# Layer 3: four of 32 tiles of exponentials summed by accumulating DMA in place of three summed by products with ones on TensorE

## The chip, the core and the metric

The kernel runs on one core of a Trainium2 chip. The core has TensorE (PE: matrix products, from SBUF into PSUM), ScalarE (ACT: here the exponentials), VectorE (DVE: elementwise sums and scalings), GpSimd (POOL: here only constants and DMA issues at the start), SyncE (SP: issues DMAs) and 16 DMA engines that all the queues share. The metric is the device time of one execution in microseconds (us), the median of several.

## The reference

Four layers run over four images of 64 x 64 pixels with 64 channels, all in float32: a self-attention over the pixels (layer 0), a convolution block (layer 1), an attention over the columns of the feature map (layer 2), and a non-local block (layer 3), which is where the change is:

```python
def _L3_conv_ref(x, g_W, g_b, phi_W, phi_b, theta_W, theta_b, w_W, w_b, gamma, beta):
    B, H, W, C = x.shape
    N = H * W
    g_x = (jnp.einsum('bhwc,cd->bhwd', x, g_W) + g_b).reshape(B, N, INNER)
    phi_x = (jnp.einsum('bhwc,cd->bhwd', x, phi_W) + phi_b).reshape(B, N, INNER)
    theta_x = (jnp.einsum('bhwc,cd->bhwd', x, theta_W) + theta_b).reshape(B, N, INNER)
    f = jnp.einsum('bnd,bmd->bnm', theta_x, phi_x)
    f = jax.nn.softmax(f, axis=-1)
    y = jnp.einsum('bnm,bmd->bnd', f, g_x).reshape(B, H, W, INNER)
    w_y = jnp.einsum('bhwd,dc->bhwc', y, w_W) + w_b
    mean = jnp.mean(w_y, axis=(0, 1, 2))
    var = jnp.var(w_y, axis=(0, 1, 2))
    w_y = gamma * (w_y - mean) * jax.lax.rsqrt(var + EPS) + beta
    return x + w_y
```

With N = 4096 and INNER = 32, each image needs a 4096 x 4096 matrix of exponentials, its products with g, and the sum of each of its rows, by which the products are divided at the end.

## The kernel before, in words

Every layer is cut into items, and a loop in `run` issues them one after another. After item i come the pieces due at i: an item's exponentials are used by products that are due one or two items later. TensorE, ACT, DVE and POOL execute their instructions in exactly the order in which this program issues them; nothing is reordered later. A semaphore wait is added wherever an instruction needs another engine's result or overwrites what another engine still reads.

Layer 3 of an image (`layer3(b)`) is 64 items in two blocks (nb = 0 and 1) of 32 tiles (mc = 0 to 31). A block holds 2048 query pixels, and a tile has the exponentials of 128 key pixels against them, 128 x 2048 numbers in one of six rotating SBUF buffers (`ep`, six buffers). For tile n:

- `scores(n)`, line 1408: eight matmuls into two PSUM slots, then two exponentials of 128 x 1024 on ACT (lines 1413 and 1414) into the tile `e`.
- `products(n)`, issued two items later. Line 1443: four matmuls of `e` with g, accumulated over the block's 32 tiles in one PSUM bank, `y`. The row sums also need every tile added up. For that there are two ways: DVE adds the tile to `esum`, a buffer in `m.tg`, which each image has for itself (lines 1434 and 1436, 128 x 2048 per add), and TensorE multiplies tiles 9, 19 and 29 by ones into a second PSUM bank, `z` (line 1429). In the very last block of the program tiles 28 to 31 take TensorE's way. Tile 0 needs no add of its own, since the add of tile 1 takes both.
- At the end of a block ACT copies `y` out of its bank (line 1449). `totals` then has TensorE multiply `esum` by ones (`sums`, line 1455), which adds the partition sums to `z`. It is due four items after the block's last tile, or two items after it where layer 2 of a later image follows (images 0 and 1, second block). A logarithm and an exponential on ACT and three DVE instructions (`newton`, lines 1471 to 1473) make the reciprocal and divide, spread over the following items; then `close`, eleven items after, projects by W (line 1490), with ACT's bias (line 1503) and the statistics for the normalisation on DVE (line 1505).

In a block that follows another of the same image, the first add of the new block (line 1434) overwrites `esum`, so it waits for the `sums` of the block before it.

`new_acc` hands out two PSUM banks in turn; a block takes one for `y` and one for `z`. `xn` is a pool with a single 128 x 2048 buffer, used by layer 1's normalisation. Layer 3 of image 0 runs after layer 2 of image 1, that of image 1 after layer 2 of image 2, and layer 3 of images 2 and 3 run one after the other at the end. During image 2's first block, pieces of preparation for image 3 (`close2`, `open3`) are put between the items; the latter issues 16 DMAs on SP (`ph<-tg`).

Of the kernel before, what the change touches and what calls it, by code (L numbers as in the profile page):

```python
# [8 lines left out]
F32 = mybir.dt.float32  # L9
AF = mybir.ActivationFunctionType  # L10
ALU = mybir.AluOpType
# [680 lines left out]
def fast_path(ctx: ExitStack, tc: tile.TileContext, a: dict, out: bass.AP, bad):  # L692
    nc = tc.nc
# [10 lines left out]
    xn = ctx.enter_context(tc.tile_pool(name="xn", bufs=1))  # L704
# [10 lines left out]
    def new_ps():  # L715
        s = turn_of["slots"][turn_of["ps"] % len(turn_of["slots"])]
        turn_of["ps"] += 1
        return PS[:, bass.ts(s, 1024)]
# [4 lines left out]
    def new_acc():  # L723
        turn_of["acc"] += 1
        return PS[:, bass.ts(6 + turn_of["acc"] % 2, 512)]

    def new_e(name="e"):
        return ep.tile([128, 2048], F32, tag="e", name=name)

    def new_t(name="t"):  # L730
        return tp.tile([128, 1024], F32, tag="t", name=name)
# [8 lines left out]
    act = nc.scalar.activation  # L740
# [9 lines left out]
    def fetch_x(b, queues):  # L750
# [17 lines left out]
        out=gam0, in_=a["L0_conv_gamma"].rearrange("(o n) -> o n", o=1).to_broadcast([128, 1])  # L768
# [44 lines left out]
    for nm in names128:  # L813
        r = flat[nm].shape[0] // 128
        nc.sync.dma_start(
            out=rows[col[nm] : col[nm] + r, :], in_=flat[nm].rearrange("(r c) -> r c", r=r)
        )
    for nm in names64 + names32:
        n = flat[nm].shape[0]
        nc.sync.dma_start(  # L820
            out=rows[col[nm] : col[nm] + 1, :].rearrange("o (d n) -> o d n", n=n),
            in_=flat[nm].rearrange("(r d n) -> r d n", r=1, d=1).to_broadcast([1, 128 // n, n]),
# [523 lines left out]


    wys, early = {}, []
    small = {}
    held = []  # L1350

# [44 lines left out]
    def layer3(b):  # L1396
        m, first, last = im[b], len(items), b == B - 1
        es, st = {}, {}

        def scores(n):  # L1400
            nb, mc = n // 32, n % 32
            e = es[n] = new_e()
            tiles = [new_ps(), new_ps()]
            for kp in range(2):
                for c in range(2):
                    for i in range(2):
                        rows_ = slice(64 * kp + 32 * i, 64 * kp + 32 * i + 32)
                        mm(  # L1408
                            tiles[kp][64 * c : 64 * c + 64, bass.ts(i, 512)],
                            m.ph[rows_, 128 * mc + 64 * c : 128 * mc + 64 * c + 64],  # L1410
                            m.th[rows_, bass.ts(nb, 512)], start=True, stop=True,
                        )
            act(e[:, 0:1024], tiles[0], AF.Exp)  # L1413
            held.append(lambda: act(e[:, 1024:2048], tiles[1], AF.Exp))  # L1414
            if not (mc == 1 and (nb or last)):
                held.pop()()
            for fn in small.get(first + n, []):
                fn()

        def products(n):  # L1420
            nb, mc = n // 32, n % 32
            e, esum = es[n], m.tg[:, 2048:4096]
            if mc == 0:
                st["y"] = new_acc()
            if mc % 10 == 9 or (last and n >= 60):
                if mc == 9:
                    st["z"] = new_acc()
                for k in range(4):
                    mm(  # L1429
                        st["z"][32 * k : 32 * k + 32, :], ones[:, 0:32], e[:, bass.ts(k, 512)],  # L1430
                        start=mc == 9, stop=False,
                    )
            elif mc == 1:
                nc.vector.tensor_add(esum, es[n - 1], e)
            elif mc:
                nc.vector.tensor_add(esum, esum, e)  # L1436
            if last and n == 62:
                return
            if last and n == 63:
                sums()  # L1440
            for i in (n - 1, n) if last and n == 63 else (n,):
                for k in range(4):
                    mm(  # L1443
                        st["y"][32 * k : 32 * k + 32, :], m.gx[:, i % 32, :], es[i][:, bass.ts(k, 512)],
                        start=mc == 0, stop=i % 32 == 31,
                    )
            if mc == 31 and not (last and n == 63):
                st["yz"] = new_t("yz")
                nc.scalar.copy(st["yz"][:, 0:512], st["y"])
                if held:  # L1450
                    held.pop()()

        def sums():
            for k in range(4):
                mm(
                    st["z"][32 * k : 32 * k + 32, :], ones[:, 0:32],
                    m.tg[:, 2048 + 512 * k : 2560 + 512 * k], start=False, stop=True,
                )


        def log(cols):
            st["inv"] = st.get("inv") or new_t("inv")
            act(st["inv"][:, cols], st["z"][:, cols], AF.Ln)

        def exp(cols):
            act(st["inv"][:, cols], st["inv"][:, cols], AF.Exp, scale=-1.0)

        def newton(nb):
            yz, z, t = st["yz"], st["z"], st.pop("inv")
            r, d = t[:, 0:512], t[:, 512:1024]  # L1470
            nc.vector.tensor_mul(d, z, r)
            stt(d, d, -2.0, r, ALU.add, ALU.mult, accum_out=inv3[:, 2 * b + nb : 2 * b + nb + 1])
            stt(yz[:, 0:512], d, -1.0, yz[:, 0:512], ALU.mult, ALU.mult)

        def totals(n):
            sums()
            steps = [
                lambda: log(slice(0, 256)), lambda: log(slice(256, 512)),
                lambda: exp(slice(0, 256)), lambda: exp(slice(256, 512)), lambda: newton(n // 32),
            ]  # L1480
            for i, fn in enumerate(steps):
                if n == 63 and b < 2:
                    fn()
                else:
                    small.setdefault(first + n + 5 + min(i, 3), []).append(fn)

        def project(yz, ps, c0, cols):
            for k in range(4):
                s, jj = k // 2, k % 2
                mm(  # L1490
                    ps[64 * s : 64 * s + 64, 512 * jj : 512 * jj + c0], wo[32 * k : 32 * k + 32, :],
                    yz[32 * k : 32 * k + 32, cols], start=True, stop=True,
                )

        def close(nb):
            if b % 2 == 0 and nb == 0:
                wys["pair"] = new_big("wy") if b else new_pad("wy")
            if nb == 0:
                wys[b] = wys["pair"][:, bass.ts(b % 2, 2048)]
            ps = new_ps()  # L1500
            project(st["yz"], ps, 512, slice(0, 512))
            wy = wys[b][:, bass.ts(nb, 1024)]
            act(wy, ps, AF.Identity, bias=V("L3_conv_w_b"))
            for i in range(2):
                nc.vector.bn_stats(bst[:, b, nb, i, :], wy[:, bass.ts(i, 512)])

        def close_last():
            yz, inv, wy = new_t("yz"), new_t("inv"), wys[b][:, 1024:2048].rearrange("p (j n) -> p j n", j=2)
            for i in range(2):
                r = inv[:, bass.ts(i, 256)]  # L1510
                act(r, st["z"][:, bass.ts(i, 256)], AF.Ln)
                act(r, r, AF.Exp, scale=-1.0)
            early.append(begin_out(0))
            for i in range(2):
                cols, r, d = bass.ts(i, 256), inv[:, bass.ts(i, 256)], inv[:, 512 + 256 * i : 768 + 256 * i]
                nc.vector.tensor_mul(d, st["z"][:, cols], r)
                k = 2 * b + 1 + i
                stt(d, d, -2.0, r, ALU.add, ALU.mult, accum_out=inv3[:, k : k + 1])
                stt(yz[:, cols], d, -1.0, st["y"][:, cols], ALU.mult, ALU.mult)
                ps = new_ps()  # L1520
                project(yz, ps, 256, cols)
                act(
                    wy[:, :, cols], ps.rearrange("p (j n) -> p j n", j=2)[:, :, 0:256],
                    AF.Identity, bias=V("L3_conv_w_b"),
                )
            for i in range(2):
                nc.vector.bn_stats(bst[:, b, 1, i, :], wy[:, :, bass.ts(i, 256)])

        for n in range(64):
            items.append((lambda n=n: scores(n), 1.0))  # L1530
            at(first + n + 2, lambda n=n: products(n))
            if last and n == 63:
                at(first + n + 2, close_last)
            elif n % 32 == 31:
                at(first + n + (2 if n == 63 and b < 2 else 4), lambda n=n: totals(n))
                at(first + n + 11, lambda n=n: close(n // 32))
# [255 lines left out]
```

## Time and profile before

| | us |
|---|---|
| median of 4 runs | 2604.98 |
| lowest to highest | 2603.13 to 2605.3 |
| the profiled execution | 2604.95 |
| its span, first to last instruction | 2603.2 |
| granted TensorE clock, mean | 0.998 of full |

Busy time of each engine in stretches of layer 3, as the profile gives it (image 0's two blocks, then image 2's second and image 3's first):

| stretch, us | length | PE | DVE | ACT | POOL |
|---|---|---|---|---|---|
| 1519 to 1588 | 69 | 69.00 | 62.39 | 59.83 | 0.00 |
| 1588 to 1665 | 77 | 77.00 | 67.27 | 68.17 | 0.00 |
| 2350 to 2430 | 80 | 80.00 | 70.40 | 70.59 | 0.00 |
| 2430 to 2500 | 70 | 70.00 | 64.16 | 61.88 | 0.00 |

In the profile's rows PE is TensorE's matmuls and PEld its weight loads. A float32 matmul shows as two records, so four matmuls are eight records. Matmuls overlap each other and their ends are modelled, so one matmul's duration is longer than its share of TensorE's time; the distance between starts tells more. ACT's exponentials overlap a little as well: two in a row are 0.92 us apart at 1.02 us each. A row of the timeline gives the start, the duration, the engine, the line, the operation with its destination and sources, and how many instructions were merged into it; in brackets stands how long the engine was idle before it, and what ended that.

### The profile page before, as it was taken

The numbers are of one execution on the slowest core, as the hardware profiler recorded it, in microseconds if no ns is written. First come the engines' busy times: TensorE is split into PE (matmuls) and PEld (weight loads), VectorE is DVE, ScalarE is ACT, GpSimd is POOL, SyncE is SP. The second block draws the span as 40 slices with busy tenths as digits, with TensorE's granted clock in tenths as the row PEclk, the third lists the DMA queues.
The fourth block names the chain that finished last, engine by engine and source line by source line (L and its number), as shares of the span: only waits on it lengthen the run. The fifth ranks groups of instructions, "written<-read, shape, count | busy, mean of one in ns | idle before, by whom it ended". The sixth has DMA issues, their size and how long they took to land.

```text
span 2603.2 us, 55344 instructions
## 1 busy us (share of the span) xinstructions
PE 2572.2 (99%) x24477; PEld 871.8 (33%) x24477; DVE 1162.7 (45%) x1302; ACT 1769.1 (68%) x2814; POOL 14.3 (1%) x46
## 2 busy tenths in 40 slices
PE   9999999999999999999999999999999999999997
PEld 3343333333333345333333322233322333322223
DVE  2010266312672237613671168610088500098996
ACT  4666766666666676666656578756688655678885
POOL 2000000000000000000000000000000000000000
PEclk9999999999999999999999999999999999999999
DMA  3000000001000000010010000010000010010002
GB/s 75 1 18 1 17 18 2 17 2 33 1 2 17 17 18 1 1 33 18 1 33 18 17 1 2 2 34 1 18 2 1 9 26 1 1 34 2 1 2 67
DMA packets 24557, 36.75 MB, mean 14 GB/s; under 512 B 3724, under 2 KB 12149, under 8 KB 24309
## 3 DMA queue, kind: packets, MB, share of 16 engines
q1 hardware_dynamic: 23285, 32.03, 5.6%
q8 instruction: 194, 3.18, 0.5%
q0 software_dynamic: 704, 0.56, 0.1%
q10 hardware_dynamic: 320, 0.54, 0.1%
q14 instruction: 54, 0.44, 0.1%
HBM read 4.80 MB, written 4.19 MB: 3 GB/s over the span
## 4 chain that ended last, share of the span: by engine, by line
PE 96%; ACT 2%; DVE 1%; issue 0%; SPq 0%; DMA 0%; ACTq 0%; DVEq 0%
PE PS L1307 17%; PE PS L1289 17%; PE PS L1084 16%; PE PS L1058 16%; PE PS L1408 11%; PE PS L1443 10%; PE PS L1168 2%; PE PS L1429 1%; ACT e L1063 1%; PE PS L1026 1%; PE PS L1230 1%; PE PS L1253 1%; PE PS L1133 1%; PE PS L1387 1%; ACT q L1008 0%; PE PS L941 0%
## 5 line engine op out<-in xcount | busy, mean ns | idle before, releaser
L1063 ACT ACTIVATE e<-PS 128x1024 f32<-128x1024 f32 x512 | 523.7, 1023 | 327.2 <-PE PS L1058 284.7
L1297 ACT ACTIVATE e<-PS 128x1024 f32<-128x1024 f32 x512 | 516.8, 1025 | 292.6 <-PE PS L1289 289.4
L1084 PE MATMUL PS<-e,vq 64*64 64x512 f32 x4096 | 540.1, 591 | 0.0
L1058 PE MATMUL PS<-X,q 64*64 64x512 f32 x4096 | 537.3, 591 | 1.8 <-DVE X L942 1.7
L1436 DVE TENSOR_TENSOR tg<-tg,e 128x2048 f32<-128x2048 f32 x213 | 488.0, 2291 | 23.9 <-ACT e L1414 5.7
L1289 PE MATMUL PS<-ko 64*64 64x512 f32 x4096 | 469.3, 591 | 2.2 <-ACT ko L1271 1.7
L1307 PE MATMUL PS<-e,X 64*64 64x512 f32 x4096 | 464.2, 591 | 0.0
L1413 ACT ACTIVATE e<-PS 128x1024 f32<-128x1024 f32 x256 | 262.6, 1026 | 84.5 <-PE PS L1408 63.7
L1201 DVE SCALAR_TENSOR_TENSOR y<-pad,vec,y 128x1024 f32<-128x1024 f32 x240 | 308.1, 1284 | 8.2 <-ACT pad L1185 1.1
L1408 PE MATMUL PS<-tg,ph 32*64 32x512 f32 x4096 | 311.1, 613 | 0.5 <-ACT e L1413 0.5
L1443 PE MATMUL PS<-e,tg 128*32 128x512 f32 x2048 | 271.9, 603 | 0.0
L1414 ACT ACTIVATE e<-PS 128x1024 f32<-128x1024 f32 x256 | 261.6, 1022 | 0.0
L1058 PEld LDWEIGHTS PS<-X,q 64*64 64x64 f32 x4096 | 161.5, 133 | 279.0 <-issue 231.6
L1289 PEld LDWEIGHTS PS<-ko 64*64 64x64 f32 x4096 | 156.8, 133 | 289.8 <-issue 199.3
L1084 PEld LDWEIGHTS PS<-e,vq 64*64 64x64 f32 x4096 | 161.1, 133 | 272.5 <-issue 170.8
L1307 PEld LDWEIGHTS PS<-e,X 64*64 64x64 f32 x4096 | 155.6, 133 | 274.9 <-issue 271.4
L1071 DVE TENSOR_REDUCE sums<-zs 128x1 f32<-128x4 f32 x128 | 19.8, 155 | 374.3 <-ACT e L1063 374.2
L1315 DVE TENSOR_TENSOR ph<-ph,PS 128x512 f32<-128x512 f32 x16 | 11.0, 687 | 391.7 <-ACT ph L1314 391.7
L1408 PEld LDWEIGHTS PS<-tg,ph 32*64 32x64 f32 x4096 | 80.6, 130 | 217.2 <-issue 119.7
L1443 PEld LDWEIGHTS PS<-e,tg 128*32 128x32 f32 x2048 | 43.6, 108 | 200.9 <-issue 196.9
L1297 ACT ACTIVATION_READ_ACCUMULATOR e<-PS 128x1 f32 x512 | 106.6, 208 | 0.0
L1063 ACT ACTIVATION_READ_ACCUMULATOR e<-PS 128x1 f32 x512 | 99.6, 195 | 0.1
(193 smaller groups left out, 948.1 us busy)
## 6 DMA issues: line engine op xcount, KB each, us to landing
xn<-t SPq DMA_DIRECT2D x64, 128.0 KB
ph<-tg SPq DMA_DIRECT2D x64, 128.0 KB
ko<-ko SPq DMA_DIRECT2D x16, 256.0 KB
xr<-in_x_dram SPq DMA_DIRECT2D x13, 256.0 KB
q<-q SPq DMA_DIRECT2D x12, 256.0 KB
out_dram<-o SPq DMA_DIRECT2D x8, 256.0 KB
out_dram<-o SPq DMA_DIRECT2D x4, 512.0 KB
xr<-in_x_dram ACTq DMA_DIRECT2D x2, 128.0 KB
```

Source lines behind the costliest of these rows:

```text
L1058: mm(ps[64 * c : 64 * c + 64, bass.ts(r, 512)], m.q[rows_, 128 * t + 64 * c : 128 * t + 64 * c + 64], x[rows_, bass.ts(g, 512)], start=Tru ...
L1063: act(es[g // 2][:, bass.ts(g % 2, 1024)], ps, AF.Exp, bias=SHIFT0, accum_out=zs[:, g : g + 1],)
L1084: ins = mm(PS[64 * s : 64 * s + 64, 2048 + 512 * j : 2560 + 512 * j], vq[rows_, :], es[j // 2][rows_, k : k + 512], start=t == 0 and i < 2 ...
L1201: stt(y1, win, wt, y1, ALU.mult, ALU.add)
L1289: mm(ps[64 * c : 64 * c + 64, bass.ts(r, 512)], m.ko[rows_, 128 * jb + 64 * c : 128 * jb + 64 * c + 64], m.ko[rows_, bass.ts(2 * ib + r, 5 ...
L1297: act(es[n, jb], ps, AF.Exp, bias=SHIFT2, accum_out=m.zs[:, jb, ib : ib + 1])
L1307: mm(acc[r][64 * c : 64 * c + 64, :], xw[rows_, jb, :], es[n, jb][rows_, bass.ts(c, 512)], start=jb == 0, stop=jb == 31,)
L1408: mm(tiles[kp][64 * c : 64 * c + 64, bass.ts(i, 512)], m.ph[rows_, 128 * mc + 64 * c : 128 * mc + 64 * c + 64], m.th[rows_, bass.ts(nb, 51 ...
L1413: act(e[:, 0:1024], tiles[0], AF.Exp)
L1414: held.append(lambda: act(e[:, 1024:2048], tiles[1], AF.Exp))
L1436: nc.vector.tensor_add(esum, esum, e)
L1443: mm(st["y"][32 * k : 32 * k + 32, :], m.gx[:, i % 32, :], es[i][:, bass.ts(k, 512)], start=mc == 0, stop=i % 32 == 31,)
```

## The change

Tiles 3, 9, 15 and 21 of each block are no longer added by an engine. POOL issues two DMAs for each (a half tile of 128 x 1024 each, directly after the exponential that makes that half), which copy tile 3 into a 128 x 2048 buffer of the pool `xn` and add tiles 9, 15 and 21 to it (`accum_op=ALU.add`). At tile 28 DVE adds this buffer to `esum`, after its add of tile 28 itself. TensorE's products with ones are left only in the last block of the program, for tiles 28 to 31; tiles 9, 19 and 29 of the other blocks lose them, and 19 and 29 are now added by DVE. Since `z` has no products before the end of a block, it takes no bank of its own: `sums` writes it, from zero, into the bank that held `y`, and a block takes one bank instead of two.

```diff
+    BY_DMA = (3, 9, 15, 21)
...
             act(e[:, 0:1024], tiles[0], AF.Exp)
+            if mc == BY_DMA[0]:
+                st["dma"] = xn.tile([128, 2048], F32, tag="xn", name="xn")
+            for h in range(2) if mc in BY_DMA else ():
+                if h:
+                    act(e[:, 1024:2048], tiles[1], AF.Exp)
+                cols = bass.ts(h, 1024)
+                if mc == BY_DMA[0]:
+                    nc.gpsimd.dma_start(out=st["dma"][:, cols], in_=e[:, cols])
+                else:
+                    nc.gpsimd.dma_start(out=st["dma"][:, cols], in_=e[:, cols], accum_op=ALU.add)
+            if mc in BY_DMA:
+                for fn in small.get(first + n, []):
+                    fn()
+                return
             held.append(lambda: act(e[:, 1024:2048], tiles[1], AF.Exp))
...
             if mc == 0:
-                st["y"] = new_acc()
-            if mc % 10 == 9 or (last and n >= 60):
-                if mc == 9:
+                st["y"] = st[nb] = new_acc()
+            if last and n >= 60:
+                if n == 60:
                     st["z"] = new_acc()
                 for k in range(4):
                     mm(
                         st["z"][32 * k : 32 * k + 32, :], ones[:, 0:32], e[:, bass.ts(k, 512)],
-                        start=mc == 9, stop=False,
+                        start=n == 60, stop=False,
                     )
             elif mc == 1:
                 nc.vector.tensor_add(esum, es[n - 1], e)
-            elif mc:
+            elif mc and mc not in BY_DMA:
                 nc.vector.tensor_add(esum, esum, e)
+            if mc == BY_DMA[-1] + 7:
+                nc.vector.tensor_add(esum, esum, st["dma"])
...
-        def sums():
+        def sums(block=None):
+            alone = block is not None
+            if alone:
+                st["z"] = st[block]
             for k in range(4):
                 mm(
                     st["z"][32 * k : 32 * k + 32, :], ones[:, 0:32],
-                    m.tg[:, 2048 + 512 * k : 2560 + 512 * k], start=False, stop=True,
+                    m.tg[:, 2048 + 512 * k : 2560 + 512 * k], start=alone, stop=True,
                 )
...
         def totals(n):
-            sums()
+            sums(n // 32)
```

## The prediction

> **What bounds the kernel now.** I read the page first: busy shares, then the chain of work that ended last.
>
> ```profile
> PE 2572.2 (99%) x24477; PEld 871.8 (33%) x24477; DVE 1162.7 (45%) x1302; ACT 1769.1 (68%) x2814; POOL 14.3 (1%) x46
> ...
> PE 96%; ACT 2%; DVE 1%; issue 0%; SPq 0%; DMA 0%; ACTq 0%; DVEq 0%
> ```
>
> TensorE sets the end over the whole span, so products taken off it should shorten the span one for one. DVE's 45% is an average over all layers, though, so next I read layer 3 alone. First TensorE's timeline in image 0's first block (columns: start, duration in us, engine, line, operation, count).
>
> ```profile
> 1537.44 1.07 PE L1429 MATMUL PS<-e,ones 128*32 128x512 f32 x8
> 1538.32 1.04 PE L1443 MATMUL PS<-e,tg 128*32 128x512 f32 x8
> ...
> 1540.34 1.07 PE L1443 MATMUL PS<-e,tg 128*32 128x512 f32 x8
> ...
> 1542.55 1.06 PE L1443 MATMUL PS<-e,tg 128*32 128x512 f32 x8
> ...
> 1544.59 1.06 PE L1443 MATMUL PS<-e,tg 128*32 128x512 f32 x8
> ...
> 1546.79 1.06 PE L1443 MATMUL PS<-e,tg 128*32 128x512 f32 x8
> ```
>
> A tile's four products with ones take 1538.32 - 1537.44 = 0.88 us of TensorE (matmuls overlap, so starts count, not durations). A tile without them takes (1546.79 - 1542.55) / 2 = 2.12 us. Next DVE's timeline in image 2's second block.
>
> ```profile
> 2356.18 2.29 DVE L1434 TENSOR_TENSOR tg<-e 128x2048 f32<-128x2048 f32 x1 [6.05 <-PE PS L1455]
> ...
> 2366.65 0.69 DVE L1471 TENSOR_TENSOR inv<-PS,inv 128x512 f32<-128x512 f32 x1 [0.99 <-ACT inv L1466]
> ...
> 2376.77 50.12 DVE L1436 TENSOR_TENSOR tg<-tg,e 128x2048 f32<-128x2048 f32 x21
> ```
>
> Twenty-one adds run back to back: the pitch is (50.12 - 2.29) / 20 = 2.39 us, more than the 2.12 us of a tile. So DVE is the slower engine on every tile that it adds, and catches up only on tiles that it skips. In this block it never waits after 2366.65. The last row is how close that comes to mattering: the end of the block, on three engines.
>
> ```profile
> 2419.00 1.02 ACT L1414 ACTIVATE e<-PS 128x1024 f32<-128x1024 f32 x1
> ...
> 2426.80 2.28 DVE L1434 TENSOR_TENSOR tg<-e 128x2048 f32<-128x2048 f32 x1
> ...
> 2427.81 1.06 PE L1455 MATMUL PS<-tg,ones 128*32 128x512 f32 x8
> ```
>
> The last exponential is ready at 2420.02. The block's last add ends at 2376.77 + 20 x 2.39 + 2.29 = 2426.9, and TensorE reads the sum at 2427.81: only 0.9 us to spare.
>
> **What the change takes away.** The products with ones, now:
>
> ```profile
> L1429 PE MATMUL PS<-e,ones x216: 592/593/618, 1537.4 to 2567.5; 128*32 128x512 f32 x108
> ```
>
> 216 records at 8 per tile are 27 tiles. Four stay (the last block's tiles 28 to 31). 23 x 0.88 = **20.2 us** go: 2.64 in each of seven blocks, 1.76 in the last.
>
> **DVE's adds.** Before, a block has 28: tiles 1 to 31 without 9, 19 and 29. After, it has 27 (without 3, 9, 15 and 21) and one more for the DMA's sum: again 28, the last block 24 for 25. The count is equal; the places are not. The skipped tile 3 lies ahead of the reciprocal (L1471), which waits for ACT (the 0.99 above), so its room is lost in waiting. From tile 8 on, DVE had 21 adds (8, 10 to 18, 20 to 28, 30, 31) and gets 22 (8, 10 to 14, 16 to 20, 22 to 31 and the extra one). They end at 2376.77 + 21 x 2.39 + 2.29 = 2429.25. Without its products TensorE comes to the sums at 2427.81 - 2.64 = 2425.17. It **waits 4.1 us**, and behind it in order stand the next block's products and scores. Image 3's first block has the same figures (2449.59 in place of 2376.77, 2500.62 in place of 2427.81): 4.1 again.
>
> Images 0 and 1 end their second block under layer 2's longer items, and the sums come later: 1665.35 - 2.64 = 1662.71, against adds that end at 1613.11 + 21 x 2.39 + 2.29 = 1665.59, so 2.9 each. There the sums now share a bank with y and also wait for ACT's copy of it (1666.03 + 0.60 - 2.64 = 1663.99); the adds end later and cover that, and without them it would cost 1.3. In the other blocks the copy is over two tiles earlier, so it costs nothing.
>
> The first blocks of images 0, 1 and 2 begin with DVE on time. The skips bring it back to no lag at tile 22 (1564.50, waiting for ACT). Then come 11 adds: 1564.50 + 10 x 2.39 + 2.29 = 1590.69, against sums at 1591.34 - 0.88 = 1590.46. 0.3 each. The last block has TensorE's four tiles at its end and waits for nothing.
>
> Given back: 2 x 4.1 + 2 x 2.9 + 3 x 0.3 = **14.9 us**. Net -20.2 + 14.9 = -5.3.
>
> DVE's lag also holds the ring of six exponential tiles, where tile n + 6 overwrites n: tile 29's add ends at 2376.77 + 19 x 2.39 + 2.29 = 2424.47, and ACT wants its buffer at 2427.51 - 2.64 = 2424.87. 0.4 to spare, so nothing.
>
> **The DMAs.** Eight per block on POOL, 0.52 MB each. POOL does nothing else in layer 3, and only the next DMA is queued behind one that waits. What can cost is the same ring: ACT's exponential of tile n + 6, with all of ACT and then the scores behind it, waits until the DMA has read n. The time it has, on ACT's timeline:
>
> ```profile
> 2406.26 1.02 ACT L1414 ACTIVATE e<-PS 128x1024 f32<-128x1024 f32 x1
> ...
> 2418.08 1.02 ACT L1413 ACTIVATE e<-PS 128x1024 f32<-128x1024 f32 x1 [0.16 <-PE PS L1408]
> ```
>
> 2418.08 - 2407.28 = 10.8 us after the second half is ready. No accumulating DMA is in the trace. Nearest are a small transfer from POOL (issue to landing in the last column) and two windows full of plain ones (the last two columns: busy share of the DMA engines, GB/s), SBUF to SBUF and stores.
>
> ```profile
> wo<-in_L_conv_w_W_dram POOLq DMA_DIRECT2D x4, 8.0 KB, 1.9
> ```
>
> ```profile
> 1302.00:1313.00 11.00, 11.00 (x105) 4.55 (x108) 9.73 (x11) 4.13 (x8) 0.00 (x0) 1.00 0.90 192
> ...
> 2583.00:2595.00 12.00, 6.57 (x55) 5.58 (x53) 8.49 (x21) 5.28 (x6) 0.00 (x0) 0.93 0.93 294
> ```
>
> Half a tile is 0.524 MB / (294 / 0.93) = 1.66 us at best, 0.524 / (192 / 0.90) = 2.46 as SBUF to SBUF. Accumulating reads a second operand: between no dearer (1.66) and three times the slower row (7.4). I take twice that row, 4.9, at most, since the plain copy has one read and one write in it and one read comes on top. The first half is ready 0.92 before the second (2419.00 - 2418.08, the exponentials' starts) and lands after 1.9 fixed; both have landed 2T + 1.0 after the tile, so **T up to 4.9 us is free**. At 1.66 the DMA gives nothing beyond that, since nothing waits. At 7.4 tiles come 15.8 - 10.8 = 5.0 late, 4.8 after ACT's 0.2 of idle (0.16 to 0.21 before an exponential), on 32 tiles: +154. The extra add is some 20 us behind tile 21's DMA and waits for none.
>
> The Trainium skill ("Collectives: The Full Stack", section on the bandwidth ceiling) says that a DMA's add costs nothing itself but needs two reads, which halves the rate. No run here shows it; by it T would be an estimated 3.3 to 4.9, and the sum stays at -5.3.
>
> POOL's issues take 0.55 us each by its rows at the start (L788); whether they hold DVE's adds up is open. Between nothing and 0.55 each; I take nothing, because DVE's two adds on L1028 at 14.47, beside POOL's issues on L848 from 13.84 to 15.35, take 1.29 us together, and so do the two like them on L1389 with POOL idle. Those have one operand in SBUF, though, and layer 3's have two.
>
> The Trainium skill ("SBUF — State Buffer", the summary and "Who interferes with whom") speaks against the change: a DMA issued by GpSimd should not be hidden under DVE work in its two-port modes. The same page excepts tensor_tensor, which takes only the read side. No row here shows either; by the warning the sum would be the third rival's, by the exception the forecast's.
>
> **Sum.** The profiled execution took 2604.95 (span 2603.2), as good as the median 2604.98. 2604.95 - 5.3 = 2599.65, which I round to **2599.5**; 1 us on each of the four large waits makes 2594 to 2605.
>
> **Rivals.**
> 1. *The full gain*: DVE's lag is absorbed. For it: 45% busy, 96% of the chain TensorE. Against: 21 adds without a gap and 0.9 us to spare. 2604.95 - 20.2 = 2584.7.
> 2. *The DMA holds the ring* (slower): ACT waits at tiles 9, 15, 21 and 27 for the DMA's read. For it: two operands, and 4.9 is just the limit. Against: the plain rows, 1.66 and 2.46. Each wait lets DVE catch up, so the 14.9 vanish: at T = 6, (13.0 - 10.8 - 0.2) x 32 = 64, so 2604.95 - 20.2 + 64 = 2649. It decides from T = 4.9; slower than before from 20.2 / 32 = 0.63 per tile, T = 5.3.
> 3. *POOL's issues hold DVE*: six of 0.55 after tile 8, 3.3 in each of four ends, some 2 in the first blocks: 2599.5 + 15 = 2615. Slower than before by the bound from about 0.4 each.
>
> That the change does nothing is excluded: 184 matmul records go.
>
> **How the numbers follow.** Forecast 0.55, full gain 0.10, ring 0.22, POOL 0.08, something unseen 0.05. This kernel's measurement can tell 0.2% (5.2 us) from no change, and the forecast lies on that line: about half of its 0.55 is faster (0.28), nearly all the rest within (0.24), 0.03 beyond. With the full gain and 0.02 of the unseen: faster 0.40. Within: 0.24 + 0.01 = 0.25. Slower: 0.03 + 0.22 + 0.08 + 0.02 = 0.35. The range goes from 2588 to 2640: outside stay the full gain (0.10) and about half of the ring's case. The forecast's own range is 2594 to 2605.
>
> **What would show it.** L1429 down to 32 records; items of 2.12 us without gaps at tiles 9 and 19; TensorE's sums line waiting for DVE 4 us twice, 3 us twice and next to nothing three times; ACT never waiting for a DMA; adds still at 2.29. Wrong if ACT's exponentials wait for DMAs, if adds stretch beside POOL's issues, or if the sums don't wait.

## The result, and the profile after

| | before | after |
|---|---|---|
| median, us | 2604.35 (59 runs) | 2608.37 (39 runs) |
| lowest to highest | 2602.57 to 2605.66 | 2607.05 to 2610.93 |
| profiled execution, us | 2604.95 | 2610.73 |
| its span, us | 2603.2 | 2608.9 |
| granted TensorE clock, mean | 0.998 | 0.994 |

The changed kernel takes 1.0017 of the time before, with a 95% interval of 1.0013 to 1.0022. It is slower by 0.17%, where 0.2% faster was forecast; the time lies inside the range. The changed kernel's runs lie in two groups, 22 from 2607.05 to 2608.48 and 17 from 2609.56 to 2610.93 (why stays open), and the profiled one is in the upper, 2.4 us above the median, so sums over the trace are made against 2610.73: +5.8 us, not the +4.0 of the medians.

The page of the changed kernel, busy time, chain of waits, the group of VectorE's adds and the DMAs:

```profile
PE 2563.5 (98%) x24293; PEld 867.9 (33%) x24293; DVE 1160.5 (44%) x1301; ACT 1770.6 (68%) x2814; POOL 65.2 (3%) x110
...
PE 85%; DVE 10%; ACT 3%; issue 1%; SPq 0%; DMA 0%; DVEq 0%; ACTq 0%
...
L1451 DVE TENSOR_TENSOR tg<-tg,e 128x2048 f32<-128x2048 f32 x204 | 467.4, 2291 | 34.7 <-ACT e L1429 16.5
...
xn<-e POOLq DMA_DIRECT2D x64, 512.0 KB, 4.5
```

The 184 matmul records are gone (24477 - 24293). But busy time fell by only 8.7 us, and the chain, which was 96% TensorE, now runs through VectorE for a tenth of the span. The adds themselves still take 2.29 us, and the DMAs (POOL's 64 issues are the rise from 46 to 110) land 4.5 us after their issue in the median of all, 3.1 for the copies of tile 3 and 6.0 for the accumulating ones. The answer for the products with ones (minimum, median and maximum in ns, first and last start) shows what stayed:

```profile
L1444 PE MATMUL PS<-e,ones x32: 592/592/617, 2568.7 to 2574.7; 128*32 128x512 f32 x32
```

The list of waits has a new entry (us in total, times, longest):

```profile
PE PS L1475 <- DVE tg L1451: 15.8, 5, 4.3
```

That is TensorE's products of the sums, the old L1455, waiting five times for VectorE. One of them on the timeline, at the end of image 2's second block:

```profile
2423.27 7.08 DVE L1451 TENSOR_TENSOR tg<-tg,e 128x2048 f32<-128x2048 f32 x3
...
2425.18 1.50 PE L1409 MATMUL PS<-tg,ph 32*64 32x512 f32 x16
...
2430.41 1.93 PE L1475 MATMUL PS<-tg,ones 128*32 128x512 f32 x8 [3.73 <-DVE tg L1451]
...
2432.12 1.93 PE L1460 MATMUL PS<-e,tg 128*32 128x512 f32 x8
...
2433.98 2.01 PE L1409 MATMUL PS<-tg,ph 32*64 32x512 f32 x16
...
2437.15 1.11 PE L1409 MATMUL PS<-tg,ph 32*64 32x512 f32 x16
...
2438.19 1.07 PE L1460 MATMUL PS<-e,tg 128*32 128x512 f32 x8
```

VectorE's last three adds end at 2430.35, and TensorE goes on 0.06 later. The wait is as forecast. What follows it is not: the same groups of matmuls that take 1.07 and 1.11 us at 2437 take 1.93 and 2.01 right behind the wait, and the distance from the sums to the products is 1.71 us (2432.12 - 2430.41), twice the 0.86 to 0.88 that four matmuls keep elsewhere. The table by stretch says why (busy us and count of PE, PEld, DVE, ACT, POOL, then the granted TensorE clock, the DMA share and GB/s):

```profile
2426.00:2430.40 4.40, 0.68 (x12) 0.00 (x0) 4.30 (x3) 2.29 (x3) 1.12 (x2) 0.91 0.34 141
2430.40:2436.00 5.60, 5.59 (x36) 1.00 (x40) 4.45 (x2) 0.00 (x0) 0.00 (x0) 0.50 0.20 80
2436.00:2442.00 6.00, 6.00 (x72) 1.36 (x72) 2.29 (x1) 5.91 (x8) 0.00 (x0) 0.96 0.00 0
```

TensorE is given half its clock, and it looks fully busy while it is: 5.59 of 5.60 us for 36 matmul records, where 6.00 us at nearly full clock hold 72. The trace's own record of the clock has five such stretches in layer 3, one behind each large wait. (The wait is the distance between starts less the 0.4 to 0.5 us that it has without one.)

| end of | wait of the sums, us | forecast | half clock from, us | for, us |
|---|---|---|---|---|
| image 0, first block | 0.16 | 0.3 | | |
| image 0, second | 3.29 | 2.9 | 1665.04 | 3.41 |
| image 1, first | 0.16 | 0.3 | | |
| image 1, second | 2.94 | 2.9 | 2043.91 | 3.41 |
| image 2, first | 1.94 | 0.3 | 2354.53 | 3.41 |
| image 2, second | 3.79 | 4.1 | 2429.62 | 6.83 |
| image 3, first | 4.38 | 4.1 | 2508.13 | 3.41 |
| sum | 16.7 | 14.9 | | 20.5 |

Half of 20.5 us is 10.2 us. TensorE was still waiting for 0.9 us of these stretches (to 2430.41 in the one from 2429.62, to 2044.04 in the one from 2043.91), so 9.8 us of its work are lost. Up to the last sums of the program the account is -20.2 + 16.7 + 9.8 = +6.3, and the trace has +7.2 (2575.53 against 2568.36, the last matmul of these sums); the 0.9 that is left stays open. The stretch from there to the end is 1.5 us shorter than before (33.3 against 34.8), which leaves the 5.7 of the spans.

### The profile page after: what moved, and what is told of

It is laid out like the page before. It is cut to its first block, busy times and chain, and to the rows that moved or that the text cites. A ratio compares the mean times of both kernels' runs of the same rounds, so it can differ in the third digit from the quotient of the medians.

```text
span 2608.9 us, 55135 instructions
## 1 busy us (share of the span) xinstructions
PE 2563.5 (98%) x24293; PEld 867.9 (33%) x24293; DVE 1160.5 (44%) x1301; ACT 1770.6 (68%) x2814; POOL 65.2 (3%) x110
## 4 chain that ended last, share of the span: by engine, by line
PE 85%; DVE 10%; ACT 3%; issue 1%; SPq 0%; DMA 0%; DVEq 0%; ACTq 0%
PE PS L1307 17%; PE PS L1084 16%; PE PS L1289 16%; PE PS L1058 16%; DVE tg L1451 9%; PE PS L1409 6%; PE PS L1460 5%; PE PS L1168 2%; ACT e L1063 1%; PE PS L1026 1%; PE PS L1230 1%; PE PS L1253 1%; PE PS L1133 1%; PE PS L1388 1%; DVE tg L1453 1%
## 5 line engine op out<-in xcount | busy, mean ns | idle before, releaser
L1063 ACT ACTIVATE e<-PS 128x1024 f32<-128x1024 f32 x512 | 524.1, 1024 | 326.9 <-PE PS L1058 284.6
L1297 ACT ACTIVATE e<-PS 128x1024 f32<-128x1024 f32 x512 | 517.1, 1025 | 292.7 <-PE PS L1289 289.4
L1451 DVE TENSOR_TENSOR tg<-tg,e 128x2048 f32<-128x2048 f32 x204 | 467.4, 2291 | 34.7 <-ACT e L1429 16.5
L1414 ACT ACTIVATE e<-PS 128x1024 f32<-128x1024 f32 x256 | 262.7, 1026 | 84.6 <-PE PS L1409 61.4
L1429 ACT ACTIVATE e<-PS 128x1024 f32<-128x1024 f32 x224 | 228.5, 1020 | 0.0
```

Of the source, the lines that this page charges most:

```text
L1063: act(es[g // 2][:, bass.ts(g % 2, 1024)], ps, AF.Exp, bias=SHIFT0, accum_out=zs[:, g : g + 1],)
L1297: act(es[n, jb], ps, AF.Exp, bias=SHIFT2, accum_out=m.zs[:, jb, ib : ib + 1])
```

## The experiments

Theory A: the change saves its 20.2 us; VectorE's lateness costs the waits, and each wait costs once more by the half clock behind it. Rivals: the DMAs or their issue on GpSimd cost something (B), and the clock falls for another reason, or only on paper (C). Times are medians; "before" is the kernel before on the same chip.

**1. Two adds less per block.** The extra add of the DMA's sum and tile 29's add are left out, and with them five tiles of the row sums in each block. All DMAs stay.

```diff
-            elif mc and mc not in BY_DMA:
+            elif mc and mc not in BY_DMA and mc != 29:
                 nc.vector.tensor_add(esum, esum, e)
-            if mc == BY_DMA[-1] + 7:
-                nc.vector.tensor_add(esum, esum, st["dma"])
```

> Leaves out of the row sums the DMA's four tiles and tile 29 (two of DVE's adds per block less, both behind tile 8); all DMAs stay. Late-sums theory (DVE's adds end after TensorE has come to the sums; TensorE waits 16.7 us in all, and its clock is halved for six stretches of 3.41 us behind the waits, which costs 10.2): both vanish, all 20.2 us of removed products are gained, 2604.4 - 20.2 = 2584. DMA theory (the 64 DMAs themselves cost the unexplained 9 us): only the 16.7 of waits go, 2608.4 - 16.7 = 2592.

Measured: 2586.47 against 2604.00, ratio 0.9933 [0.9917, 0.9950]. No wait for VectorE is left and the clock is whole up to the tail. TensorE's only new wait in layer 3 is the one for ACT's copy of the shared bank:

```profile
PE PS L1473 <- ACT yz L1464: 2.3, 2, 1.2
```

That is the 1.3 at each of two ends that the prediction named as covered by VectorE's lateness; here the cover is gone. 2604.0 - 20.2 + 2.6 = 2586.4. So nothing that belongs to the DMAs costs time, and the whole loss hangs on VectorE's lateness.

**2. The DMAs alone.** The kernel before, plus the 64 DMAs of the changed one, whose sum is not used.

```diff
+            if mc == BY_DMA[0]:
+                st["dma"] = xn.tile([128, 2048], F32, tag="xn", name="xn")
...
+                    nc.gpsimd.dma_start(out=st["dma"][:, cols], in_=e[:, cols], accum_op=ALU.add)
```

> The kernel before, with the 64 DMAs of the change issued besides and their sum read by nobody. Late-sums theory: DMAs are free, 2604.4 within 1 us, no wait of ACT for a DMA, clock 0.998. DMA theory: about 9 us more, 2613.

Measured: 2603.79 against 2604.00, ratio 0.9998 [0.9988, 1.0008]. B falls.

**3. The waits filled.** Before each late sum TensorE gets products that nobody reads, in groups of four, as many as the wait is long. They take the place of the wait and save no time by themselves.

```diff
+    FILL = (0, 3, 0, 3, 2, 4, 4, 0)
...
+                for k in range(4 * FILL[2 * b + block]):
+                    mm(
+                        st["z"][32 * (k % 4) : 32 * (k % 4) + 32, :], ones[:, 0:32],
+                        X[:, 0, bass.ts(k % 4, 512)], start=True, stop=True,
+                    )
```

> The changed kernel with products without use (ones by image 0's features) ahead of the sums, so that TensorE works while DVE finishes: 4 groups of 0.88 us at the ends of image 2's second and image 3's first block, 3 at those of images 0 and 1, 2 at image 2's first. If the clock falls because TensorE stands idle: it stays full, waits shrink to under 1 us each, and 10 us are saved although TensorE has 14 us more to do: 2608.4 - 10.2 = 2598. If the clock falls for another reason (the DMAs, power): no gain, 2608 or above.

Measured: 2602.26 against 2604.00, ratio 0.9994 [0.9984, 1.0003]; 6.1 us under the changed kernel. The table by stretch around the same end:

```profile
2426.00:2431.00 5.00, 4.84 (x52) 0.96 (x48) 4.90 (x3) 1.04 (x2) 0.00 (x0) 1.00 0.38 152
2431.00:2436.00 5.00, 5.00 (x64) 1.19 (x60) 2.79 (x2) 5.00 (x7) 0.00 (x0) 1.00 0.01 3
```

More work for TensorE, and the program is faster, since the clock stays at 1.00. C falls: the half clock is real, and idleness brings it. The gain is less than the 10.2 expected for reasons that the traces show: at the ends of images 0 and 1 the filler writes the shared bank and first waits 1.3 us for ACT's copy, so that it ends 0.6 and 1.0 us too late (the sums start 11.99 and 12.00 us after the block's last tile, against 11.35 and 11.00); the median of the changed kernel lies 2.4 under its profiled run; and the half clock cost 9.8, not 10.2.

**4. The same four tiles, later.** The tiles are 9, 15, 21 and 27, so that VectorE catches up nearer the end; the extra add comes at tile 31 (28 in the last block). The number of adds is that of the changed kernel.

```diff
-    BY_DMA = (3, 9, 15, 21)
+    BY_DMA = (9, 15, 21, 27)
...
-            if mc == BY_DMA[-1] + 7:
+            if mc == (28 if last and nb else 31):
```

> The changed kernel with tiles 9, 15, 21 and 27 by DMA in place of 3, 9, 15 and 21, and the DMA's sum added at tile 31 (28 in the last block): as many adds, but 21 instead of 22 behind tile 8. Late-sums theory: each large wait is 2.39 us shorter, 1.4 + 2.0 + 0.9 + 0.6 are left, 4.9 in all, none long enough to halve the clock: 2604.4 - 20.2 + 4.9 = 2589. If only the number of adds counted: 2608, as the change.

Measured: 2591.76 against 2604.00, ratio 0.9954 [0.9937, 0.9970]. It is where the tiles stand that decides, not how many they are. Four waits remain, 1.3 and 1.3 for the shared bank and 1.63 and 1.99 for VectorE, and TensorE's timeline around the last two shows a border between them:

```profile
2413.01 1.49 PE L1409 MATMUL PS<-tg,ph 32*64 32x512 f32 x16
2416.06 1.07 PE L1475 MATMUL PS<-tg,ones 128*32 128x512 f32 x8 [1.56 <-DVE tg L1453]
2416.94 1.04 PE L1460 MATMUL PS<-e,tg 128*32 128x512 f32 x8
...
2484.88 1.50 PE L1409 MATMUL PS<-tg,ph 32*64 32x512 f32 x16
2488.31 1.60 PE L1475 MATMUL PS<-tg,ones 128*32 128x512 f32 x8 [1.93 <-DVE tg L1453]
2489.66 1.96 PE L1460 MATMUL PS<-e,tg 128*32 128x512 f32 x8
```

Behind 1.63 us the products take 1.04 as always; behind 1.99 they take 1.96, for one stretch of 3.41 us at 2488.70. The account: 2604.0 - 20.2 + 6.3 + 1.7 = 2591.8. It misses the expected 2589 by the 1.7 of a half clock that was not expected behind 2.0 us, and by the shared bank, which costs 1.3 at the ends of images 0 and 1 where 0.9 and 0.6 were expected.

**5. The waits made shorter, not filled.** Experiment 3 with a group of four fewer at five of its six ends.

```diff
-    FILL = (0, 3, 0, 3, 2, 4, 4, 0)
+    FILL = (0, 2, 0, 2, 1, 3, 4, 0)
```

> The kernel with filler products ahead of the sums (2602.3), with one group of four fewer at five of its six ends: (2, 2, 1, 3, 4) groups at the second blocks of images 0 and 1, the first and second of image 2 and the first of image 3. TensorE is then left waiting for VectorE for 1.5, 1.2, 1.1, 1.2 and 0.9 us by the waits of the changed kernel less 0.88 a group. In all traces so far the clock's full and half stretches are whole multiples of 3.41 us, and a window of 3.41 us was followed by a half one when at least 1.94 us of it were a wait, never when 1.63 or less were. If that is what decides, all five waits leave the clock whole, and the time is that of the kernel with filler less its overshoot at two ends (0.6 + 1.0): 2600.6, in any case not above 2602.5. If any wait of a microsecond or more halves the clock, five times 1.7 us come on top: 2609.

Measured: 2601.05 against 2604.28, ratio 0.9988 [0.9979, 0.9997]. The waits for VectorE that remain are 1.2 us at most by the distance of the starts, at three ends; at those of images 0 and 1 the filler waits 1.3 us for the shared bank instead. The clock is 1.00 throughout layer 3. The list of waits (us in total, times, longest) has the three for VectorE:

```profile
PE PS L1481 <- DVE tg L1452: 2.6, 3, 1.0
```

So short waits cost their length and no more. This kernel is the changed one without its half clock: 2604.35 - 20.2 + 16.7 = 2600.9, against 2601.05.

**6. Six tiles by DMA.** Tiles 5, 9, 13, 17, 21 and 25, with the extra add at 29: 26 adds per block instead of 28.

```diff
-    BY_DMA = (3, 9, 15, 21)
+    BY_DMA = (5, 9, 13, 17, 21, 25)
...
-            if mc == BY_DMA[-1] + 7:
+            if mc == BY_DMA[-1] + 4:
```

> The changed kernel with six tiles by DMA (5, 9, 13, 17, 21, 25) and the DMA's sum added at tile 29: 26 adds a block in place of 28, and none of the skipped tiles ahead of the reciprocal. Late-sums theory: TensorE never waits for DVE and its clock stays full; what is left is the wait for ACT's copy in the shared bank at the ends of images 0 and 1, 1.3 each: 2604.2 - 20.2 + 2.6 = 2586.6. If DMAs at four tiles' distance hold the ring: above 2595, with ACT waiting for DMAs.

Measured: 2590.72 against 2603.85, ratio 0.9948 [0.9934, 0.9961]. No wait for VectorE, none of ACT for a DMA, the clock whole, the two waits for the shared bank back. It is 4.1 over the expectation, of which 3.1 are at the very end of the program (below) and 1.0 stays open.

**7. Six tiles, and the sums in a bank of their own** where the sums follow ACT's copy closely, that is in the second blocks of images 0 and 1.

```diff
-                st["z"] = st[block]
+                st["z"] = new_acc() if block and b < 2 else st[block]
```

> As the kernel with six tiles, but the sums at the ends of images 0 and 1 go into the other bank. If the shared bank costs 1.3 at each of these ends: 2.6 less, 2584. If that wait is hidden anyway: the same as with six tiles, within 0.5.

Measured: 2587.34 against 2603.85, ratio 0.9937 [0.9923, 0.9950]; 3.4 under experiment 6, where 2.6 were expected. No wait is left at any sum. It is again some 3 us over.

**8. The DMA's sum multiplied by ones on TensorE** instead of added by VectorE. This one miscarried. (The diff shows the main piece; VectorE's extra add is left to the last block alone, and the sums then add to what these products wrote.)

```diff
+                if not (last and block):
+                    for k in range(4):
+                        mm(
+                            st["z"][32 * k : 32 * k + 32, :], ones[:, 0:32],
+                            st["dma"][:, bass.ts(k, 512)], start=True, stop=False,
+                        )
```

> The changed kernel, but the DMA's sum is multiplied by ones on TensorE at the sums instead of added by DVE (not in the last block): 0.88 us more for TensorE in seven blocks, 2.39 less for DVE. Late-sums theory: waits of 0.8 and 1.1 at the ends of image 2's second and image 3's first block, 1.3 each for the shared bank at those of images 0 and 1, clock full: 2604.2 - 20.2 + 6.2 + 4.5 = 2595. If only TensorE's work counted: 2608 + 6.

Measured: 2622.26 against 2603.85, ratio 1.0067 [1.0053, 1.0080].

```profile
PE PS L1476 <- DMA xn<-e: 15.7, 4, 3.9
```

In the four blocks that another block of the same image follows, the next block's tile 3 has been issued by the time of the sums, and the name then stands for the next block's buffer: TensorE waits 3.9 us for a DMA that it should not need, and its values are the wrong block's. So the run says nothing on what it was made for. It does show that the half clock does not care what TensorE waits for: each of these four waits is followed by 3.41 or 6.83 us of it.

**9 to 11. Where the last 3 us of experiments 6 and 7 are.** In every kernel here TensorE ends 24.5 us after the last sums; but the span ends 33.3 to 33.7 after them with 64 DMAs and 36.4 with 96 (and 34.8 in the kernel before, without any of them). The trace shows a DRAIN on GpSimd's queue at the end of the program, 4.02 and 6.76 us long. Three variants of experiment 7: five tiles (without 25); six tiles with one DMA of 1 MB per tile; five tiles so. The diff is that of one DMA per tile.

```diff
-            for h in range(2) if mc in BY_DMA else ():
-                if h:
-                    act(e[:, 1024:2048], tiles[1], AF.Exp)
-                cols = bass.ts(h, 1024)
+            if mc in BY_DMA:
+                act(e[:, 1024:2048], tiles[1], AF.Exp)
                 if mc == BY_DMA[0]:
-                    nc.gpsimd.dma_start(out=st["dma"][:, cols], in_=e[:, cols])
+                    nc.gpsimd.dma_start(out=st["dma"], in_=e)
                 else:
-                    nc.gpsimd.dma_start(out=st["dma"][:, cols], in_=e[:, cols], accum_op=ALU.add)
+                    nc.gpsimd.dma_start(out=st["dma"], in_=e, accum_op=ALU.add)
```

> Five tiles of a block go by accumulating DMA instead of six (80 DMAs instead of 96; tile 25 is added by VectorE again, so 27 adds per block), the rest as in the kernel with six tiles and z's own bank (2587.3). In that kernel the computing tail after the last sums is as long as everywhere (TensorE ends 24.5 us behind them), but GpSimd's DRAIN at the end of the program takes 6.76 us with 96 DMAs, 4.02 with 64, and the span ends 36.4 us behind the sums instead of 33.3. If the drain grows with the DMAs, it is 5.4 us here and the end comes some 1.4 earlier: 2586, provided that VectorE, which has one add more per block, still ends ahead of the sums. If the one add more makes TensorE wait again, about 1 to 2 us at each of four blocks with a half clock behind it: 2592 or more. If the longer end has nothing to do with the DMAs: 2587.3.

> The kernel with six tiles and z's own bank, with one DMA of 1 MB per tile instead of two of 512 KB (48 DMAs, the same bytes). If the drain at the end goes by the number of DMAs it is some 2.6 us and is hidden behind SP's end as in the kernels with 64: 2584. If it goes by bytes or packets it stays 6.8: 2587.3. If the later start of the first half's DMA holds the ring of exponentials (both halves wait for the second half's exponential, about 1 to 2 us later, and 1 MB lands later than 512 KB), ScalarE waits for a DMA at some of the 47 tiles and the time rises by up to 1 us for each: over 2590.

> Both: five tiles, one DMA of 1 MB each (40 DMAs). If the drain goes by the number of DMAs, it is hidden and the time is that of six tiles with one DMA each, 2584, as long as VectorE's one add more causes no wait; by bytes, 5.4 us of drain, 2586.

| kernel | DMAs | time, us | ratio, 95% interval | DRAIN, us | last sums to end of span, us |
|---|---|---|---|---|---|
| experiment 7 | 96 of 512 KB | 2587.34 | 0.9937 [0.9923, 0.9950] | 6.76 | 36.4 |
| five tiles | 80 of 512 KB | 2587.99 | 0.9936 [0.9923, 0.9950] | 5.41 | 35.0 |
| six, one DMA each | 48 of 1 MB | 2586.45 | 0.9931 [0.9917, 0.9944] | 5.78 | 35.2 |
| five, one DMA each | 40 of 1 MB | 2587.13 | 0.9933 [0.9920, 0.9947] | 5.12 | 34.4 |

Fewer DMAs of one size mean a shorter drain, 1.35 us for 16 of 512 KB. But half as many of double size save only 1.0, so it goes neither by number nor by bytes alone, and what it goes by stays open. Five tiles win 1.5 at the end and lose it again: with one add more per block VectorE is late by 0.2 to 0.6 us at five ends. One DMA per tile holds nothing up; ACT waits for none. The page of six tiles with one DMA each, the fastest complete kernel here, though within the interval of the others:

```profile
PE 2553.7 (99%) x24293; PEld 867.0 (34%) x24293; DVE 1124.7 (44%) x1285; ACT 1768.9 (68%) x2814; POOL 53.6 (2%) x94
...
PE 96%; ACT 2%; DVE 1%; issue 0%; SPq 0%; DMA 0%; DVEq 0%; ACTq 0%
...
xn<-e POOLq DMA_DIRECT2D x48, 1024.0 KB, 6.9
```

The chain is TensorE's again. It is 0.7% faster than the kernel before.

## Why the prediction was wrong, step by step

- **Products removed, 20.2 us: right.** Experiment 1 is 17.5 under its kernel before, 20.1 with the two bank waits added back.
- **VectorE's lateness, 14.9 us: right as a mechanism, 1.8 short.** The four large waits, forecast as 14.0, came to 14.4. The miss is image 2's first block, 1.94 instead of 0.3. The prediction took image 0's figures for it; but there VectorE also does the preparation for image 3 between the adds, and falls behind. Its last idle moment is at 2325.8, and from there it has 12 adds in a row to the sums, not the 11 of image 0.
- **What a wait costs: this is the step that failed.** The prediction charged TensorE's waits by their length, and made its net -5.3 from -20.2 + 14.9. It left out that TensorE comes back from a wait with half its clock. With the right waits and no more the sum would be -3.5, and experiment 5 shows that kernel at 2601.05, 1.5 from the forecast. The changed kernel is 7.3 above it (medians), 9.6 by the profiled runs (2610.73 - 2601.18), for a computed 9.8. That term alone turned a gain into a loss. A trace of it stood in the prediction's own quotation: the tail window of the kernel before, quoted for its DMA share, has TensorE busy for 6.57 of 12 us and a granted clock of 0.93.
- **The DMAs, nothing: right.** No exponential waits for one, and the accumulating ones land in a median of 6.0 us from issue (4.4 to 7.8). Experiment 2 shows them free. One packet of 4 KB of an accumulating DMA takes 328 ns on its engine, so a half tile with eight on each of 16 engines is 2.6 us; the assumed 4.9 was cautious, and 2.6 is also under the 3.3 to 4.9 that the prediction estimated with a halved rate. The halving itself is there: a packet of the plain copies of tile 3 takes 159 ns.
- **POOL's issues beside VectorE's adds, nothing: right.** 2.29 us per add as before, though an accumulating issue takes 0.87 us and not the 0.55 assumed; of the two rules that the prediction quotes, the exception for tensor_tensor held and not the warning.
- **The ring, 0.4 to spare, nothing: right.** No exponential in layer 3 waits for VectorE.
- **The bank shared by y and z, 1.3 if uncovered: right,** by experiments 1 and 7.
- **The rivals.** The full gain, the ring held by DMAs and the issues that hold VectorE did not come. None of the cases held the clock; it was in the 0.05 of the unseen. That the time lies inside the stated range is luck: its upper part was there for the ring and for POOL's issues. The forecast's own range was also added up too wide: 1 us on each of four waits gives 2595.5 to 2603.5 around 2599.5, not 2594 to 2605.

The Trainium skill ("TensorE: Matmul & The Clock Gate", sections on what is happening and on why this matters for kernels) has a rule that was missing: an idle window of about 3.4 us brings TensorE to half rate, the window runs on its own, and idle gaps should not exceed some 3 us. The window's length and its running on its own agree with the stretches of 3.41 us here. The border does not: waits of 1.94, 1.99 and 2.94 us, within it, each brought half a clock. With the page's border the term would have been an estimated 1.7 us, half of one window, for each of the two waits forecast above 3 us (4.1 each).

## What to carry to other kernels

A wait of the engine that sets the end is not priced by its length where that engine is TensorE: here every wait from 1.9 us up cost up to another 1.7 us for each window of half clock behind it, and none up to 1.6 did, so cut the wait below that or keep TensorE busy. When work goes from the busiest engine to another whose pitch per item is only just above its own, count the items after the last moment at which that engine has caught up, in each place separately, and choose the items that it is spared close to the deadline: here four tiles chosen a few places later made 16 us of difference. And measure the clock beside the busy share, since TensorE at half clock shows as fully busy.

## What the runs showed of the hardware

- **The clock goes by a fixed grid of windows.** In the changed kernel the half and full stretches from the first half one on are 1, 110, 1, 90, 1, 21, 2, 21, 1 and 26 times 3.413 us, up to the tail, and in experiments 4 and 8 they are whole multiples too. With the waits laid on that grid (0.45 us taken off for the distance of starts without a wait), what share of a window was a wait explains all that was seen in layer 3 (without the tail behind the last sums) in the changed kernel and in experiments 1, 4, 5, 6 and 8:

| wait within a window, us | clock in it | clock in the next | cases |
|---|---|---|---|
| up to 1.70 | full | full | all |
| 1.83 to 3.08 | full | half | 10 of 10 |
| 0.79 to 2.24 | half | half | 4 of 4 |
| 0 to 0.13 | half | full | all |

  The border lies between 1.70 and 1.83 us, about half a window; a half window was followed by a full one only when at most 0.13 us of it were a wait. By this, where a wait falls on the grid should count as well as its length; no run was made to test that.
- **An accumulating DMA's packet takes about twice a plain one's:** 328 ns against 159 for the 4 KB packets of the copies of tile 3 and of the stores at the end. GpSimd spends 0.87 us on issuing one, against 0.56 for the copy.
- **DMAs that GpSimd issues have a price at the end of the program,** in the DRAIN of its queue, after all of them have long landed: 1.86 us before, 4.02 with the change, where it ends with SP's last work (2607.73 and 2607.74) and the program ends no later than before, and 6.76 with 96 DMAs, where the program ends 3.1 us later after the last sums than with 64, and 1.6 later than before the change.
